# Head and tail of an attention layer: x loaded and summed first, and three products of the last but one group kept in PSUM

## The chip, the cores and the metric

The kernel runs on one core of a Trainium2 chip. The metric is device time in microseconds (us) of one execution. A core has a matrix engine (TensorE, PE in the profile, with PEld for its weight loads), a vector engine (VectorE, DVE), a scalar engine (ScalarE, ACT), GpSimd (POOL) and SyncE (SP). Each takes its own instructions in order; SP, ACT and POOL also issue DMAs. Matrix products are written to PSUM, a small memory of eight banks; everything else lies in SBUF.

## The reference

Input x is 8 x 256 x 512 in fp32. All that matters of the computation:

```python
xn = layernorm(x)                                   # over the last axis, eps 1e-5
q, k, v = xn @ wq.T, xn @ wk.T, xn @ wv.T           # 32 heads, 8 key/value heads of 128
q, k = rotary(q), rotary(k)
scores = q @ k.T / sqrt(128) * key_scale + causal   # 256 x 256 for each head
s = softmax(scores) @ v @ wo.T
logits = xn @ router_w.T                            # 4 experts, the best 2 of them kept
delta = sum_e gate_e * ((xn @ A_e.T) @ B_e.T) * 4   # rank 16
out = x + s * silu(delta)
```

## The kernel before

**Tiling.** Batches are taken two at a time: `tb` runs over 4 pairs (512 rows of x, four tiles of 128 rows), `g` over 8 groups of four heads, `b` over the two batches of a pair. Every large product (query, key, value, output projection) is done by a scheme of seven products in place of eight for a 2 x 2 block matrix (Strassen's, in Winograd's form). Its operands are blocks A11, A12, A21, A22 and sums of blocks S1 to S4 (S3 is written over A21), on both sides. One such set of weights is called a quad; 12 quads for each `tb` give queries, keys and values. Products of a quad are p1, p2, p6, p5, p7, p4, p3, each of four `nc.tensor.matmul` of 128 x 128 by 128 x 256, which are eight instructions in the profile.

**Head.** `norm(0)` (lines 318 to 478) loads four tiles of x through SP, takes mean and variance on VectorE (`statistics`, `variance`), the root on ScalarE (`root`), the reciprocal (`invert`) and the normalised tile (`normalise`) on VectorE, in two slices of two tiles. TensorE turns them (`turn`, one job for both tiles of a batch and one half of the columns; tile `xp`), ScalarE copies them out of PSUM (`read`; XB), and VectorE makes the four sums of x that the scheme needs (`add_up`; XT). `turn` serves the first pair only; later pairs are turned by VectorE and DMAs. Before it, TensorE multiplies the identity by itself (`warm`, line 1380). Weights of the first two quads come through SP (`blocks_of`, lines 482 to 545), those of all later ones through POOL; sums of weight blocks (`sum_up`, w<-w,w in the profile) are made on VectorE in the first pair and stored to DRAM by POOL (`keep_sum`, sums<-w) for the other three pairs. The router's products (`route`, four pieces, tile `lm`) and its weights (`ra`) belong to the head too. Weight tiles live in a ring of 9 (`w`) and 8 (`wo`), whose places are taken in a fixed turn.

**Middle.** For each group and batch: scores on TensorE (`sc`), softmax on VectorE and ScalarE, the probabilities turned by VectorE and two rounds of DMAs through DRAM (`there`, then `pT`), probabilities times values (`av`), and the output projection (`out_project`, line 930, `po`). The output projection has seven products for each group, and each product k has its own accumulator `acc[tb, k]` in SBUF, to which VectorE adds the product of each group (`add_up`, line 973; acc<-acc,po). Products take one of four PSUM banks tagged `mm`.

**Tail.** For the last pair's last group, `last_products` (line 1008) first adds accumulators into each other (`put`, seven sums in one chain), makes one of the four quarters of the output ready (`prepare(4, 1, 0)`: times gate, plus x), then runs the last seven products in PSUM banks `oa`, `oe`, `od` and two for halves of the seventh; ScalarE copies `oa` aside three times (p1, u2, u3), VectorE adds `oe` or `od` to these (`bank_and`), and `result` makes each quarter (plus accumulator, times gate, plus x: three operations), which SP stores.

**What sets the order.** All work is entered in a plan as jobs with an engine, an estimated duration, predecessors (`after`), rooms that they open and close (buffers of a tag, `Room` and `Hold`) and sometimes a job that they should be near to. The order of TensorE's jobs is laid out by hand (`lay`, lines 1362 and 1399 to 1446), which gives each a due time; due times of the other jobs are worked back from it (`Plan.run`, line 199), a job with `near` also taking that job's time as a limit. The plan then plays time forward with the estimated durations: whenever an engine is free, the ready job with the earliest due time, whose rooms have space, is emitted (jobs due more than 30 us after the earliest TensorE job not yet started are held back). A ready job with a late due time runs if nothing else is ready. The order found so is the program order of each engine on the chip; the waits there are real ones.

Nearly every instruction is recorded under line 118 (the helper that emits in program order), so tiles are named by their tensors in the profile.

## Time and profile before

| | us |
|---|---|
| runs of the kernel before | 1341.76, 1347.17, 1347.25 (median 1347.17) |
| the profiled execution | 1345.25 |
| its span, first to last instruction | 1343.5 |
| TensorE busy in the span | 1325.6 |
| VectorE busy in the span | 1102.8 |
| waits of TensorE for turned probabilities (`av` for `pT`) | 8.2, in 7 waits |
| start of the first product that needs a sum of x (`pdk<-XT,w`) | 15.94 |
| end of the last matmul | 1337.3 |
| end of VectorE's last operation | 1340.1 |

The profile is one execution. A line of the timeline gives start, time of the whole run of instructions, engine, operation, written and read tensors, and in brackets the engine's idle time just before it with what ended it. PE times are modelled at their ends: products that follow each other without a gap start 1.73 us apart, while a row of eight instructions shows 1.89 to 1.99.

### The profile page before, as it was taken

How to read it: one execution, taken by the hardware profiler on the slowest of the kernel's cores; microseconds unless marked ns; L12 is line 12 of the kernel's file. 1: busy time of each engine (PE TensorE's matmuls, PEld its weight loads, DVE VectorE, ACT ScalarE, POOL GpSimd, SP SyncE). 2: the span in 40 equal slices, each digit the busy share in tenths (PEclk: the TensorE clock that was granted, in tenths of full speed). 3: DMA queues.
4: the chain of work that ended last, by engine and by line, in shares of the span. 5: the costliest groups of instructions: out<-in, count | busy, mean ns of one | idle time of the engine just before them, and what ended most of it. 6: DMA issues, size and time to landing. Idle time of an engine off the chain costs nothing.

```text
span 1343.5 us, 19943 instructions
## 1 busy us (share of the span) xinstructions
PE 1325.6 (99%) x6488; PEld 1167.2 (87%) x6488; DVE 1102.8 (82%) x2835; ACT 611.2 (45%) x1576; POOL 314.3 (23%) x579
## 2 busy tenths in 40 slices
PE   9999999999999999999999999999999999999998
PEld 8888888888889888888888988888888898888886
DVE  6899989997978769788697875969868787686997
ACT  3474454543534435354353453535444454534531
POOL 2332232222222122221222212222122222222010
PEclk9999999999999999999999999999999999999999
DMA  6588677596766766768666676576876676666484
GB/s 212 165 264 253 203 217 226 197 261 205 244 178 199 223 202 185 232 210 221 205 223 202 214 208 216 175 236 210 227 221 191 220 219 205 191 189 199 137 282 135
DMA packets 134182, 282.10 MB, mean 210 GB/s; under 512 B 40832, under 2 KB 80896, under 8 KB 134080
## 3 DMA queue, kind: packets, MB, share of 16 engines
q0 software_dynamic: 45760, 149.98, 36.3%
q1 hardware_dynamic: 88096, 130.19, 31.7%
q8 instruction: 52, 0.85, 0.3%
q10 hardware_dynamic: 224, 0.66, 0.2%
q14 instruction: 50, 0.41, 0.1%
HBM read 197.94 MB, written 82.84 MB: 209 GB/s over the span
## 4 chain that ended last, share of the span: by engine, by line
PE 80%; DVE 10%; DMA 6%; SPq 2%; issue 1%; ACT 1%; DVEq 0%; ACTq 0%
PE po L118 21%; PE paq L118 15%; PE av L118 10%; PE sc L118 8%; PE pdq L118 7%; DMA pT<-there 5%; PE peq L118 4%; PE pak L118 4%; PE pav L118 4%; PE pdk L118 2%; SPq L118 2%; PE pdv L118 2%; DVE blocks L118 2%; DVE qTq L118 1%; DVE p L118 1%; DVE acc L118 1%
## 5 line engine op out<-in xcount | busy, mean ns | idle before, releaser
L118 ACT ACTIVATE p<-z,least 128x256 f32<-128x256 f32 (+7 forms) x512 | 207.6, 406 | 199.0 <-DVE least L118 130.3
L118 PE MATMUL po<-wo,a 128*128 128x256 f32 x992 | 233.0, 379 | 0.0
L118 PEld LDWEIGHTS po<-wo,a 128*128 128x128 f32 x992 | 186.7, 190 | 22.9
L118 PE MATMUL av<-pT,v 128*128 128x256 f32 x768 | 185.5, 380 | 8.2 <-DMA pT<-there 8.2
L118 PE MATMUL paq<-XT,w 128*128 128x256 f32 x768 | 182.0, 380 | 0.0
L118 DVE CUSTOM_DVE_ANT_0 z<-sc,tab 128x256 f32<-128x256 f32 (+7 forms) x512 | 134.1, 300 | 57.1 <-PE sc L118 54.1
L118 PE MATMUL po<-wo,s 128*128 128x256 f32 x744 | 177.6, 382 | 0.2 <-PE av L118 0.2
L118 PEld LDWEIGHTS av<-pT,v 128*128 128x128 f32 x768 | 145.0, 190 | 30.1 <-DMA pT<-there 6.1
L118 PEld LDWEIGHTS sc<-kk,qTq 128*128 128x128 f32 x1024 | 159.2, 191 | 12.6 <-DVE p L118 0.8
L118 PE MATMUL sc<-kk,qTq 128*128 128x256 f32 (+7 forms) x1024 | 168.0, 302 | 0.1
L118 PEld LDWEIGHTS paq<-XT,w 128*128 128x128 f32 x768 | 144.9, 190 | 19.5 <-ACT u2q L118 0.8
L118 POOL DMA_DIRECT2D w<-sums x144 | 79.2, 550 | 348.0 <-PE paq L118 143.9
L118 PEld LDWEIGHTS po<-wo,s 128*128 128x128 f32 x744 | 139.4, 190 | 23.4 <-issue 5.5
L118 ACT COPY a<-av 128x512 f32<-128x512 f32 x128 | 74.1, 580 | 180.8 <-PE av L118 180.6
L118 DVE TENSOR_TENSOR acc<-acc,po 128x512 f32<-128x512 f32 x189 | 127.7, 676 | 33.8 <-PE po L118 32.4
L118 ACT COPY swq<-cq 64x1024 f32<-64x1024 f32 x128 | 133.7, 1044 | 14.8 <-DVE cq L118 10.7
L118 POOL DMA_DIRECT2D w<-in_wquad_dram x148 | 80.9, 548 | 244.4 <-PE paq L118 84.6
L118 DVE STREAM_TRANSPOSE blocks<-p 128x1024 f32<-128x1024 f32 (+1 forms) x128 | 123.7, 968 | 0.4 <-DMA there<-blocks 0.2
L118 DVE TENSOR_SCALAR p<-p,total 128x256 f32<-128x256 f32 (+7 forms) x512 | 117.2, 294 | 2.3
L118 DVE TENSOR_TENSOR qTq<-cq,tab 128x1024 f32<-128x1024 f32 x64 | 77.9, 1218 | 26.2 <-ACT cq L118 26.0
L118 ACT ACTIVATION_READ_ACCUMULATOR p<-z,least 128x1 f32 x512 | 95.8, 187 | 0.0
L118 POOL DMA_DIRECT2D wo<-in_woquad_dram x104 | 56.9, 548 | 132.5 <-PE po L118 122.3
(137 smaller groups left out, 1853.3 us busy)
## 6 DMA issues: line engine op xcount, KB each, us to landing
there<-blocks SPq DMA_DIRECT2D x256, 192.0 KB, 3.8
pT<-there SPq DMA_DIRECT2D x64, 768.0 KB, 6.1
w<-in_wquad_dram POOLq DMA_DIRECT2D x148, 256.0 KB, 4.7
w<-sums POOLq DMA_DIRECT2D x144, 256.0 KB, 4.1
wo<-in_woquad_dram POOLq DMA_DIRECT2D x104, 256.0 KB, 5.0
wo<-osums POOLq DMA_DIRECT2D x96, 256.0 KB, 4.7
sums<-w POOLq DMA_DIRECT2D x48, 256.0 KB, 4.4
osums<-wo POOLq DMA_DIRECT2D x32, 256.0 KB, 4.7
```

What stands on the lines that cost most here:

```text
L118: ins = what(*args, **kwargs)
```

## The change

In the head:

- x tiles 2 and 3 are issued on SP after the first weight block (A11) instead of after the second.
- `variance` and `invert` are folded into `statistics` and `normalise`: the same instructions, in other jobs. Statistics and normalising jobs of one slice are put in a chain.
- The transposes of batch 0 are split by tile: those of tile 0, for both halves, may start when tile 0 is normalised. Estimated durations of these jobs are lower.
- The first sum of x waits for two of the four copies instead of all.
- Weight sums of the first quad are tied (`near`) to its product p3 instead of p1; in the other quads of the first pair to p1, as before.
- The four pieces of batch 0's transposes are laid ahead of the first product.

In the tail:

- Products 1, 2 and 5 of the last pair's last but one group (`fuse`) are not added to their accumulators. They stay in their PSUM banks, which become `oa`, `oe` and `od` of `last_products`, and the last group's products are accumulated on them.
- The order of that group's products becomes 1, 2, 6, 7, 5, 3, 4, and that of the last group 1, 5, 6, 2, 7, first half of 3, 4, second half of 3.
- The sums of accumulators are no longer one chain. All four quarters are prepared (times gate, plus x) ahead; `result` then multiplies the bank's value by the gate and adds the prepared accumulator.

The core of the diff:

```diff
-        def statistics(t):
+        def statistics(t, ts):
...
+            if t == ts.stop - 1:
+                nc.vector.tensor_scalar_add(box["r"][:, ts], box["mv"][:, ts, 1], EPS)
...
-        def normalise(t):
+        def normalise(t, ts):
+            if t == ts.start:
+                nc.vector.reciprocal(box["r"][:, ts], box["r"][:, ts])
...
             sts = [
-                add("dve", 0.9, lambda t=t: statistics(t), after=[loads[t]] + xn[-1:])
+                add("dve", 0.87, lambda t=t, ts=ts: statistics(t, ts),
+                    after=[loads[t]] + sts[-1:] + (xn[-1:] if t > 1 else []))
...
+            before, h = [], ph[2 * b + half]
+            if b == 0:
+
+                for f in range(2) if half == 0 else ():
+                    pieces.append(
+                        add("pe", 0.27, lambda f=f: turn(0, f, (0,)), after=[xn[0], identity],
+                            opens=[ph[f]], closes=mh[:1])
+                    )
+                before = [pieces[half]]
+            ts = (1,) if before else (0, 1)
...
-        t1 = add("dve", 0.61, lambda: add_up(0), after=reads)
-        t2 = add("dve", 0.61, lambda: add_up(1), after=[t1])
+        t1 = add("dve", 0.61, lambda: add_up(0), after=reads[0:3:2])
+        t2 = add("dve", 0.61, lambda: add_up(1), after=[t1] + reads)
...
-            if lead and k == 1:
+            if lead and k == 0:
                 plan.then(issue[0], first[2])
                 issue = first[3:]
...
-        if not tb:
-            for i in Features.sums:
-                sums_of["w", which, i].near = (p1, 0.0)
...
+        if not tb:
+
+            of = p1 if len(weights) > 1 else p3
+            for i in Features.sums:
+                sums_of["w", which, i].near = (of, 0.0)
...
+        fuse = (tb, g) == (NTB - 1, KV - 2)
...
+            if fuse and k in (1, 2, 5):
+
+                fused[k] = box, h, p
+                pieces[k] = p
+                return
...
-        return [pieces[k] for k in (1, 2, 6, 5, 7, 4, 3)]
+        return [pieces[k] for k in ((1, 2, 6, 7, 5, 3, 4) if fuse else (1, 2, 6, 5, 7, 4, 3))]
...
-        prepare(4, 1, 0)
+        for k, b, f in ((2, 0, 0), (3, 0, 1), (5, 1, 1), (4, 1, 0)):
+            prepare(k, b, f)
...
-            r = dve(
-                lambda: nc.vector.tensor_add(s(), s(), box[what]), turn + [first, M[k]["done"]]
-            )
-            m = dve(lambda: gate(s(), s(), b, f), [r, loads["g", b]])
+            m = dve(lambda: gate(box[what], box[what], b, f), [first, loads["g", b]])
             return dve(
-                lambda: nc.vector.tensor_add(s(), s(), box["xf", b][:, :, bass.ts(f, 2 * P)]),
-                [m, loads["xf", b]],
-            )
...
+                lambda: nc.vector.tensor_add(M[k]["s"], M[k]["s"], box[what]), [m, M[k]["done"]]
+            )
...
-        oa, oe, od, o3, o4 = (hold("mm") for _ in range(5))
-        p1 = product("oa", A11, A11, True, [], [oa])
+        oa, oe, od = (fused[k][1] for k in (1, 2, 5))
+        for k, bank in ((1, "oa"), (2, "oe"), (5, "od")):
+            fused[bank] = fused[k]
+        o3, o4 = (hold("mm") for _ in range(2))
+        p1 = product("oa", A11, A11, False, [])
...
-        return [p1, p2, p6, p5, p7, half(0, o3, p7), p4, half(1, o4, p4)]
+        return [p1, p5, p6, p2, p7, half(0, o3, p7), p4, half(1, o4, p4)]
...
-    lay(tiles[:2] + lead[:1] + tiles[2:] + lead[1:7] + route + lead[7:14] + turn + lead[14:])
+    lay(tiles[:4] + lead[:1] + tiles[4:] + lead[1:7] + route + lead[7:14] + turn + lead[14:])
```

More of the change, by code (lines that the diff above doesn't have):

```diff
@@ L341, in statistics @@
             nc.vector.bn_aggr(out=box["mv"][:, t, :], in_=st)
-        def variance(ts):
-            nc.vector.tensor_scalar_add(box["r"][:, ts], box["mv"][:, ts, 1], EPS)
+            if t == ts.stop - 1:
+                nc.vector.tensor_scalar_add(box["r"][:, ts], box["mv"][:, ts, 1], EPS)
         def root(ts):
             nc.scalar.sqrt(box["r"][:, ts], box["r"][:, ts])
-        def invert(ts):
-            nc.vector.reciprocal(box["r"][:, ts], box["r"][:, ts])
-        def normalise(t):
+        def normalise(t, ts):
+            if t == ts.start:
+                nc.vector.reciprocal(box["r"][:, ts], box["r"][:, ts])
             xn = box[t] = two.tile([P, D], F32, tag="m", name=f"xn{tb}_{t}")
@@ L357, in normalise, with turn @@
             )
-        def turn(b, half):
-            pt = box["p", b, half] = ps_mm.tile([P, 2, S], F32, tag="mm", name=f"xp{b}_{half}")
-            for t in range(2):
+        def turn(b, half, ts):
+            if ts[0] == 0:
+                box["p", b, half] = ps_mm.tile([P, 2, S], F32, tag="mm", name=f"xp{b}_{half}")
+            for t in ts:
                 for c in range(2):
                     nc.tensor.transpose(
-                        pt[:, c, bass.ts(t, P)], box[2 * b + t][:, bass.ts(2 * half + c, P)], ident
+                        box["p", b, half][:, c, bass.ts(t, P)], box[2 * b + t][:, bass.ts(2 * half + c, P)], ident
                     )
@@ L427, in norm @@
             begun.extend(issues)
-        xn = []
+        xn, sts = [], []
         for ts in [slice(0, NT)] if tb else [slice(0, 2), slice(2, NT)]:
@@ L432, in norm @@
             sts = [
-                add("dve", 0.9, lambda t=t: statistics(t), after=[loads[t]] + xn[-1:])
+                add("dve", 0.87, lambda t=t, ts=ts: statistics(t, ts),
+                    after=[loads[t]] + sts[-1:] + (xn[-1:] if t > 1 else []))
                 for t in tiles
             ]
-            v = add("dve", 0.1, lambda ts=ts: variance(ts), after=sts)
-            r = add("act", 2.8 if tb else 0.2, lambda ts=ts: root(ts), after=[v])
-            inv = add("dve", 0.1, lambda ts=ts: invert(ts), after=[r])
+            r = add("act", 2.8 if tb else 0.2, lambda ts=ts: root(ts), after=sts)
             for t in tiles:
                 xn.append(
-                    add("dve", 0.45, lambda t=t: normalise(t), after=[inv], opens=[mh[t]],
-                        closes=[xh[t // 2]])
+                    add("dve", 0.45, lambda t=t, ts=ts: normalise(t, ts), after=[r] + xn[-1:],
+                        opens=[mh[t]], closes=[xh[t // 2]])
                 )
@@ L456, in norm @@
         for b, half in [] if tb else ((0, 0), (0, 1), (1, 0), (1, 1)):
+            before, h = [], ph[2 * b + half]
[7 more added lines that the diff above has]
+            ts = (1,) if before else (0, 1)
             tp = add(
-                "pe", 0.9, lambda b=b, h=half: turn(b, h), after=xn[2 * b : 2 * b + 2] + [identity],
-                opens=[ph[2 * b + half]], closes=mh[2 * b : 2 * b + 2],
+                "pe", 0.27 * len(ts), lambda b=b, h=half, ts=ts: turn(b, h, ts),
+                after=xn[2 * b : 2 * b + 2] + [identity] + before,
+                opens=[] if before else [h], closes=mh[2 * b + ts[0] : 2 * b + 2],
             )
@@ L462, in norm @@
                 add("act", 0.5, lambda b=b, h=half: read(b, h), after=[tp] + reads[:1],
-                    opens=[] if reads else [x_hold[tb]], closes=[ph[2 * b + half]], near=(tp, 0.5))
+                    opens=[] if reads else [x_hold[tb]], closes=[h], near=(tp, 0.5))
             )
             pieces.append(tp)
-        t1 = add("dve", 0.61, lambda: add_up(0), after=reads)
-        t2 = add("dve", 0.61, lambda: add_up(1), after=[t1])
+        t1 = add("dve", 0.61, lambda: add_up(0), after=reads[0:3:2])
+        t2 = add("dve", 0.61, lambda: add_up(1), after=[t1] + reads)
         t3 = add("dve", 0.61, lambda: add_up(2), after=reads)
@@ L764, in values_of @@
         return pieces
-    free_p = [None]
+    fused = {}
     def softmax(tb, g, b):
@@ L1013, in last_products, with put @@
         dve = lambda what, after, **kw: add("dve", 0.61, what, after=after, **kw)
-        turn = []
-        def put(to, a, b):
-            turn[:] = [
-                dve(lambda: nc.vector.tensor_add(M[to]["s"], M[a]["s"], M[b]["s"]),
-                    turn + [M[k]["done"] for k in (to, a, b)])
-            ]
-            M[to]["done"] = turn[0]
-        for to, a, b in ((2, 1, 2), (6, 1, 6), (7, 6, 7), (3, 3, 5), (3, 3, 6), (4, 7, 4), (5, 7, 5)):
-            put(to, a, b)
+        puts = []
+        def put(to, a, b, after=()):
+            M[to]["done"] = dve(
+                lambda: nc.vector.tensor_add(M[to]["s"], M[a]["s"], M[b]["s"]),
+                [M[k]["done"] for k in (to, a, b)] + list(after),
+            )
+            puts.append(M[to]["done"])
+        put(2, 1, 2)
+        put(3, 3, 5)
+        read5 = puts[-1:]
+        put(6, 1, 6)
+        put(3, 3, 6)
+        put(7, 6, 7)
+        put(5, 7, 5, read5)
+        put(4, 7, 4)
         box, loads = {}, {}
@@ L1049, in prepare @@
             s = lambda: M[k]["s"]
-            m = dve(lambda: gate(s(), s(), b, f), [M[k]["done"], turn[0], loads["g", b]])
+            m = dve(lambda: gate(s(), s(), b, f), [M[k]["done"], loads["g", b]])
             M[k]["done"] = dve(
@@ L1054, in prepare @@
             )
-        prepare(4, 1, 0)
+        for k, b, f in ((2, 0, 0), (3, 0, 1), (5, 1, 1), (4, 1, 0)):
+            prepare(k, b, f)
         banks = {}
         def product(bank, a, w, first, after, opens=(), ts=(0, 1)):
+            before = fused.get(bank)
+            along = before and bank not in banks
+            if along:
+                banks[bank] = None
+                after = after + [before[2]]
             def work():
-                if first:
+                if along:
+                    banks[bank] = before[0]["ps"]
+                elif first:
                     banks[bank] = ps_mm.tile([P, 2, 2 * P], F32, tag="mm", name=f"{bank}{n}")
@@ L1097, in result @@
         def result(k, b, f, what, first):
-            s = lambda: M[k]["s"]
-            r = dve(
-                lambda: nc.vector.tensor_add(s(), s(), box[what]), turn + [first, M[k]["done"]]
-            )
-            m = dve(lambda: gate(s(), s(), b, f), [r, loads["g", b]])
-            return dve(
-                lambda: nc.vector.tensor_add(s(), s(), box["xf", b][:, :, bass.ts(f, 2 * P)]),
-                [m, loads["xf", b]],
-            )
-        oa, oe, od, o3, o4 = (hold("mm") for _ in range(5))
-        p1 = product("oa", A11, A11, True, [], [oa])
+            m = dve(lambda: gate(box[what], box[what], b, f), [first, loads["g", b]])
+            return dve(
+                lambda: nc.vector.tensor_add(M[k]["s"], M[k]["s"], box[what]), [m, M[k]["done"]]
+            )
+        oa, oe, od = (fused[k][1] for k in (1, 2, 5))
[3 more added lines that the diff above has]
+        p1 = product("oa", A11, A11, False, [])
         c1 = aside("p1", p1)
-        p2 = product("oe", A12, A21, True, [], [oe])
+        p6 = product("oa", S2, S2, False, [c1])
+        c6 = aside("u2", p6)
+        p2 = product("oe", A12, A21, False, [p6])
         e = bank_and("p1", "oe", [p2, c1], [oe])
         store(lambda: M[2]["s"], 0, 0, p2, [result(2, 0, 0, "p1", e)])
-        p6 = product("oa", S2, S2, False, [c1])
-        c6 = aside("u2", p6)
-        p5 = product("od", S1, S1, True, [], [od])
+        p5 = product("od", S1, S1, False, [])
         d = bank_and("u2", "od", [p5, c6], [od])
@@ L1125, in last_products @@
         m = dve(
-            lambda: gate(M[7]["s"], banks["oa"], 1, 0), [p4, M[7]["done"], turn[0], loads["g", 1]],
+            lambda: gate(M[7]["s"], banks["oa"], 1, 0), [p4, M[7]["done"], loads["g", 1]] + puts,
             closes=[oa],
@@ L1136, in half @@
                 lambda: gate(M[6]["s"][:, t, :], banks[bank][:, t, :], 0, 1, t),
-                [p, M[6]["done"], turn[0], loads["g", 0]], closes=[h],
+                [p, M[6]["done"], loads["g", 0]] + puts, closes=[h],
             )
```

## The prediction

> **What bounds the kernel now.** I read the page first (busy times, chain), then who waited for whom on TensorE, then the timeline of the first 20 us and of the last 45 us.

> The page's busy times and the chain that ended last, by engine:

> ```profile
> PE 1325.6 (99%) x6488; PEld 1167.2 (87%) x6488; DVE 1102.8 (82%) x2835; ACT 611.2 (45%) x1576; POOL 314.3 (23%) x579
> ...
> PE 80%; DVE 10%; DMA 6%; SPq 2%; issue 1%; ACT 1%; DVEq 0%; ACTq 0%
> ```

> TensorE is busy for 1325.6 of 1343.5 us, so at most 17.9 us can be had without taking matmuls away, and the change takes none away. Where these 17.9 us lie, the list of TensorE's waits says (us in total, times, longest):

> ```profile
> PE av L118 <- DMA pT<-there: 8.2, 7, 1.8
> PE warm L118 <- POOL ident masks.py:199: 1.4, 1, 1.4
> PE pdk L118 <- DVE XT L118: 1.0, 1, 1.0
> PE xp L118 <- DVE xn L118: 0.6, 2, 0.5
> PE pak L118 <- ACT XB L118: 0.2, 1, 0.2
> ```

> 8.2 us are waits for turned probabilities in the middle; the last three lines, 1.9 us, are the head; the rest is the tail, 1337.3 (last matmul) to 1343.5. The head, in the timeline:

> ```profile
> 6.90 1.09 PE L118 MATMUL xp<-ident,xn 128*128 128x128 f32 x8 [0.46 <-DVE xn L118]
> 7.59 1.07 ACT L118 COPY XB<-xp 128x512 f32<-128x512 f32 x2 [1.99 <-PE xp L118]
> 8.23 1.99 PE L118 MATMUL pak<-XB,w 128*128 128x256 f32 x8 [0.24 <-ACT XB L118]
> 8.61 0.69 DVE L118 BATCH_NORM_STATS2 st<-x 128x6 f32<-128x512 f32 x1 [1.76 <-DMA x<-in_x_dram]
> 11.98 2.61 DVE L118 TENSOR_TENSOR w<-w,w 128x512 f32<-128x512 f32 x4
> 15.11 1.28 DVE L118 TENSOR_TENSOR XT<-XB 128x512 f32<-128x512 f32 x2
> 15.94 1.96 PE L118 MATMUL pdk<-XT,w 128*128 128x256 f32 x8 [0.99 <-DVE XT L118]
> ```

> VectorE waits 1.76 us for the third x tile, then does four weight sums (2.61 us) before the first sum of x (XT) at 15.11, and TensorE waits for that. The tail:

> ```profile
> 1317.41 0.69 DVE L118 TENSOR_TENSOR acc<-acc,po 128x512 f32<-128x512 f32 x1 [3.42 <-PE po L118]
> 1319.14 0.69 DVE L118 TENSOR_TENSOR acc<-acc,po 128x512 f32<-128x512 f32 x1 [1.04 <-PE po L118]
> ...
> 1336.29 1.03 PE L118 MATMUL o<-wo,s 128*128 128x256 f32 x4
> ...
> 1339.10 1.01 DVE L118 TENSOR_TENSOR acc<-acc,acc 128x512 f32<-128x512 f32 x2
> ```

> VectorE idles 3.42 + 1.04 + 0.31 + 1.04 = 5.8 us between 1314 and 1322.6, then runs without a gap over 0.4 us to 1340.1, 2.8 us after the last matmul. After the last half product only two operations of 0.42 us and a 0.2 us hop are unavoidable (0.95 us: 1338.2), so 1.9 us of the tail are VectorE's backlog.

> **The head, step by step** (p1, p2, ... are the seven products of the first quad, 1.73 us apart in the trace).
> *Transposes by tile.* The same 16 transposes (0.137 us each). Those of x tile 0 need its normalised tile, done at 6.38, and the warming matmuls end at 6.44; four transposes run 6.44 to 7.0, beside the normalising of tile 1 (done 6.84). For the first copy two more remain, 7.0 to 7.25, plus the 0.14 us seen between transposes and copy: 7.4 for 7.59. So p1 starts at 8.03, p2 at 9.76, and TensorE is free at 11.5: 0.2 us earlier.
> *Loads.* On SP the order becomes x0, x1, A11, x2, x3, A12, ra, A21, A22 (ra is ready while A21 still waits one hop for A12). Landings before, issue plus time to landing: A11 6.7, A12 7.95, x2 8.6, x3 9.25, A21 10.0, ra 10.3, A22 10.9. I give x2 the place of A12, 7.95 (at best 7.3, one spacing of 0.65 behind A11), x3 8.6, A12 9.25. The chain from first statistics to the last normalised tile took 8.61 to 12.06 = 3.45, so that tile is done at 11.43, in time for TensorE at 11.5. A12 is wanted at 9.76: 0.5 us of cover. A21 is late by ra's 0.35, hidden, as the first weight sum needs A22 too. Epsilon and reciprocal move inside other jobs, same instructions: nothing.
> *Sums of x first.* The due times no longer pull the weight sums forward, so by the planner's rules VectorE does S1, the first output sum (needs p2), S2 and the first x sum in this order. x sum 0 needs only two of the four copies: transposes 11.5, copy 12.2 to 12.8. With 0.61 us a sum from 11.45: S1 12.05, output sum 12.65, S2 13.25, x sum 13.87, p5 at 14.0 instead of 15.94. But before, two router pieces (16 matmuls in 1.90) ran ahead of p5 and now one does; the other, 0.9, follows later, in a wait that the trace shows filled anyway. Gain 1.94 - 0.9 = 1.0; with x2 at 7.3 it is 1.3. I take 1.1.
> *What is moved behind.* S3 and S4 come up to 1.8 us later (three x sums ahead); on POOL the four stores of sums follow them and nobody waits for these. SP's next two weight loads wait for ring slots that S3 and S4 free (SP waited 5.1 us for VectorE there); their sums ran at 19.86 and are used by the product at 29.98, and VectorE is busy 7.4 of 10.5 us from 16 to 26.5: hidden. If the two table loads (0.96 us of ACT's queue, 10.55 to 11.51) fall between the copies of x, copy 3 is up to 0.5 late; it feeds x sum 1, which has all of p5 (1.73) as cover.
> Bounds of the head: 0, if A12 lands as late as A22 did, 10.9, 1.1 after it is wanted; 1.9, if every wait of TensorE's head goes.

> **The tail, step by step.** Count VectorE's operations from the first product of group (3,6) on. Before: 7 adds of its products, 7 sums of accumulators, 4 sums of the last group's activations, 2 for one prepared result, 3 bank sums, 9 for three results: 32, and six for the last two results. After: 4 adds (products 1, 2, 5 stay in PSUM), 7, 4, 8 for four prepared results, 3, and 6: 32 again, and the same six. So nothing is saved; operations move. Two of product 1's and 2's adds leave the busy stretch before 1313, and "prepare result 2" (2) fills the idle one.
> TensorE after 1312.8, no wait assumed: av (2.6), products 7, 5, 3 to 1320.5, p1 to 1322.2, av to 1324.8, product 4 to 1326.5, p5, p6, p2, p7, half, p4, half to 1337.2, where it ended before.
> VectorE: product 3's add at 1320.7, then three accumulator sums and two prepared results, 8 x 0.605 to 1325.6; four activation sums, product 4's add, its accumulator sum and prepared result, 8 x 0.605 from 1325.86 to 1330.7; bank sum and result 3, 2, 5, nine x 0.605 to 1336.2; then four halves at 0.335 and two whole at 0.605 to 1338.8, for 1340.1. Gain 1.3. The last store behind it (3.4 us to the end) is the same.
> *The added wait.* Three of the four "mm" banks are held from product 5 on. Product 4 must wait for product 3's add: 0.2 from matmul to add, 0.69 the add, 0.1 back, 0.97 in all. Its cover is p1 (needs a bank that is held already, an activation copied at 1315 and a weight issued at 1305.07) and the av behind it, whose pT was issued at 1315.41 and took 5.7: there at 1321.1. Were neither ready, products 3 and 4 would both wait: 1.9 us, TensorE ends at 1339.2, VectorE 0.95 later, at 1340.1 as before: gain 0. Upper bound 1.9, the whole backlog.
> [...] No row here shows a wait for a bank, and four pieces of other work stand ready, so I go by the rows.

> **The sum.** 1.1 + 1.3 = 2.4. The profiled execution took 1345.25 (span 1343.5 and 1.75 around it): 1342.85. The timed runs are 1341.76, 1347.17 and 1347.25, their median 1.9 above the profiled one; from the middle of the four, 1346.2, the forecast is 1343.8.

> **Rivals.**
> *The middle is put in another order, for the worse (other side).* The planner lays all engines' orders out once, and the head shifts its start. The middle holds seven waits for pT, 8.2/7 = 1.17 us each, at 60 to 120, 240 to 400, 600 to 700, 900 to 1000 us, where VectorE is 93% busy at first (222.6 of 240 from 60 to 300). For it: a later probability sum is late there at once. Against it: from the second quad on no cost or due time changes but a common shift. Each more costs 1.17; from the third more (3.5 over 2.4) the kernel is slower: four give 1346.2 - 2.4 + 4.7 = 1348.5. Over 0.5% takes eight.
> *The middle for the better.* Four fewer: 1346.2 - 2.4 - 4.7 = 1339.1.
> *A gain is eaten.* A12 late, or the bank waits showing: 1346.2 - 1.1 or - 1.3, about 1345; both eaten, 1346.2: the change then does nothing.

> **How the numbers follow.** Forecast 0.5; one or both gains eaten 0.2; middle worse 0.18; middle better 0.12. 0.5% of 1347.17 is 6.7 us, about what a measurement here can tell from none, as the three runs already lie 5.5 apart: the bounds are 1340.4 and 1353.9. Faster: middle better, 0.12, and 0.08 from low runs of the forecast: 0.2. Slower: half of "worse" at the most, 0.1. Same 0.7. Range: both upper bounds (3.8) and four waits fewer, 1346.2 - 3.8 - 4.7 = 1337.7; no gain and four more, 1350.9.

> **What would show it.** Head: third x tile's statistics at 7.3 to 8.0; first XT sum before S3 and S4, near 13.3; pdk near 14.0 after one router piece. Tail: no add for products 1, 2, 5; no idle of TensorE for a bank after 1315; VectorE's last operation within 1.8 us of the last matmul. Wrong if pek waits for A12, if TensorE shows gaps of 1 us before products 3 or 4, or if the pT waits leave 8.2 by more than 3 us.

## The result, and the profile after

The changed kernel is slower. Its median is 1347.06 us against 1343.94 us for the kernel before in the same session; the ratio is 1.0024, with a 95% interval from 1.0014 to 1.0034. The forecast was 2.4 us faster; the measurement is some 3.1 us slower, inside the given range and on the other side of no change. In absolute time the forecast started too high: its base was 1346.2, from the four runs there were, and 20 runs of before have their median at 1343.94.

The profiled execution took 1350.06 us, its span is 1348.3 us, against 1345.25 and 1343.5 before. Each profile is one execution, and the time differs from execution to execution (the 20 runs of after lie between 1342.97 and 1352.23 us): the profiled one of after is 3.0 us above its median, the one of before 1.3. So the profiles show where time goes, and the timed runs how much. The page's busy times and the chain that ended last, after:

```profile
PE 1327.3 (98%) x6488; PEld 1167.4 (87%) x6488; DVE 1103.1 (82%) x2835; ACT 612.1 (45%) x1576; POOL 315.1 (23%) x579
...
PE 76%; DVE 11%; DMA 8%; SPq 2%; ACT 1%; issue 1%; DVEq 0%; ACTq 0%
```

Read the first line against the span. TensorE's matmuls, the same 6488, take 1327.3 us instead of 1325.6: 1.7 us more. Its idle time is 1348.3 - 1327.3 = 21.0 us instead of 17.9: 3.1 us more. Together these are the 4.8 us between the two spans. The chain has less TensorE in it and more DMA (8% for 6%), so the idle time hangs on transfers. TensorE's list of waits says which (us in total, times, longest):

```profile
PE av L118 <- DMA pT<-there: 11.2, 8, 2.7
PE xp L118 <- DVE xn L118: 0.9, 1, 0.9
PE pak L118 <- ACT XB L118: 0.5, 1, 0.5
PE pdk L118 <- DVE XT L118: 0.3, 1, 0.3
```

The head's wait for the sums of x (`pdk` for XT) went from 1.0 to 0.3 us, as the edit meant. The waits for turned probabilities, pT, went from 8.2 to 11.2 us: almost all of the added idle time.

**The head did what was forecast.** Its timeline, after:

```profile
7.31 0.69 DVE L118 BATCH_NORM_STATS2 st<-x 128x6 f32<-128x512 f32 x1 [0.37 <-DMA x<-in_x_dram]
13.15 1.28 DVE L118 TENSOR_TENSOR XT<-XB 128x512 f32<-128x512 f32 x2
13.89 1.99 PE L118 MATMUL pdk<-XT,w 128*128 128x256 f32 x8 [0.34 <-DVE XT L118]
20.94 0.69 DVE L118 TENSOR_TENSOR ck<-pdk,u3k 128x512 f32<-128x512 f32 x1 [4.09 <-ACT u3k L118]
25.36 1.94 PE L118 MATMUL paq<-XB,w 128*128 128x256 f32 x8
```

The third x tile's statistics start at 7.31 (8.61 before), the first XT sum at 13.15 (15.11), `pdk` at 13.89 (15.94). All four router pieces are done in both kernels when q's first product `paq` starts, at 25.36 against 26.53: 1.17 us gained, and the first scores start 1.14 us earlier (46.8 for 48.0; here and below the second matmul of a unit's scores is taken). The fourth line is what I had not counted: VectorE now idles 4.09 us at 17 to 21 us and does work later that it did there, above all the second quad's weight sums (19.86 to 23.0 before, 25.35 to 29.6 after). From there the written-out order of every engine differs. Job for job, leaving out the first normalisation, 56 of TensorE's jobs, over 200 of VectorE's and 48 of POOL's stand in another place with the head's edits; with the tail's edits alone it is about ten, under 40 and none.

**The lead is gone at 78 us.** The first, second and fourth lines here are stores and loads on POOL, `there` and `pT` the two DMAs on SP that turn the probabilities, `av` their use; timeline of after:

```profile
58.37 1.15 POOL L118 DMA_DIRECT2D sums<-w  x2
59.52 1.64 POOL L118 DMA_DIRECT2D w<-in_wquad_dram  x3
61.05 3.55 SPq L118 DMA_DIRECT2D there<-blocks  x4
62.76 1.61 POOL L118 DMA_DIRECT2D osums<-wo  x3 [0.32 <-issue]
72.89 0.34 SPq L118 DMA_DIRECT2D pT<-there  x1
78.51 1.78 PE L118 MATMUL av<-pT,v 128*128 128x256 f32 x5 [2.71 <-DMA pT<-there]
```

The same transfers in the timeline of before:

```profile
67.64 3.09 SPq L118 DMA_DIRECT2D there<-blocks  x4
74.14 0.34 SPq L118 DMA_DIRECT2D pT<-there  x1
82.72 1.46 PE L118 MATMUL av<-pT,v 128*128 128x256 f32 x6
```

Before, the gather (`pT`) goes out 3.4 us after the last block store was issued (70.73 to 74.14) and its use comes 8.6 us later, without a wait. After, the stores go out 6.6 us earlier, into a pile of transfers of 256 KB each, and the gather goes out 8.3 us after the last of them (64.60 to 72.89). The planner allows 3.4 us for this step (its lag) in either case, and put the use ahead of the next unit's scores (a unit is one group of heads of one batch, written (tb, g, b)), where before had it behind the first of them: TensorE stands for 2.71 us. The stretches of the two kernels between 60 and 70 us, and the one behind the wait (us, busy time of each engine with its instructions, granted clock, DMA share, GB/s), after and then before:

```profile
60.00:70.00 10.00, 10.00 (x53) 9.04 (x52) 8.38 (x27) 5.74 (x15) 3.86 (x8) 1.00 0.98 320
76.10:79.50 3.40, 0.99 (x4) 0.91 (x5) 3.40 (x5) 0.33 (x1) 2.37 (x5) 0.97 0.87 306
79.50:82.90 3.40, 3.40 (x10) 2.66 (x10) 0.55 (x1) 0.59 (x1) 0.00 (x0) 0.53 0.85 240
```

```profile
60.00:70.00 10.00, 10.00 (x52) 8.19 (x52) 8.04 (x32) 6.08 (x16) 0.00 (x0) 1.00 0.35 119
```

The DMA engines are 98% busy instead of 35%. And behind the wait, from 79.5 to 82.9, TensorE is granted about half its clock (0.53): ten matmuls, where before has 19 in the same stretch. That is the 1.7 us of added busy time. A second wait, 2.43 us at 112, follows; before waits 1.53 us there. By 130 us the lead of 1.14 is a lag of 4.7 us; later waits, which before has at 290 to 390 us (1.33, 0.90, 1.83) and after nearly not (0.67), give most of it back: behind 390 us after is 1.1 us late. Up to the last unit's scores it falls to 4.1 us late again, partly by longer waits at 974 us (1.63 for 0.81) and 1176 us (0.57 for none).

**The tail** keeps TensorE's forecast order to the job, and no product waits for a bank: behind 1300 us TensorE's list of waits has 1.6 us for pT and 0.2 us of `po` for `av`, and nothing else. But the last gather does not come in time; after:

```profile
1304.84 0.71 SPq L118 DMA_DIRECT2D xf<-in_x_dram  x1
1305.60 0.86 SPq L118 DMA_DIRECT2D g<-gates  x1
1306.57 0.38 SPq L118 DMA_DIRECT2D xf<-in_x_dram  x1
1307.61 0.33 SPq L118 DMA_DIRECT2D pT<-there  x1
1318.24 2.83 PE L118 MATMUL av<-pT,v 128*128 128x256 f32 x12 [1.61 <-DMA pT<-there]
1341.77 1.03 PE L118 MATMUL o<-wo,s 128*128 128x256 f32 x4
1343.93 1.02 DVE L118 TENSOR_TENSOR acc<-acc,acc 128x512 f32<-128x512 f32 x2
```

VectorE ends 2.15 us behind TensorE (2.8 before), so its backlog shrank, though not to the 1.8 at most that was forecast. But three loads of 512 KB now stand on SP just ahead of the gather, which takes 10.5 us to land (7.4 before), and TensorE waits 1.61 us for it (0.28 before). The same gather and its use, before:

```profile
1305.33 0.33 SPq L118 DMA_DIRECT2D pT<-there  x1
1312.82 2.83 PE L118 MATMUL av<-pT,v 128*128 128x256 f32 x12 [0.28 <-DMA pT<-there]
```

From the last unit's first scores to the end of the span it is 51.6 us (50.9 before): the tail's gain is more than eaten.

### The profile page after: what moved, and what is told of

It reads as the page before. It is cut to its first block, busy times and chain, and to the rows that moved or that the text cites. A ratio compares the mean times of both kernels' runs of the same rounds, so it can differ in the third digit from the quotient of the medians.

```text
span 1348.3 us, 19942 instructions
## 1 busy us (share of the span) xinstructions
PE 1327.3 (98%) x6488; PEld 1167.4 (87%) x6488; DVE 1103.1 (82%) x2835; ACT 612.1 (45%) x1576; POOL 315.1 (23%) x579
## 4 chain that ended last, share of the span: by engine, by line
PE 76%; DVE 11%; DMA 8%; SPq 2%; ACT 1%; issue 1%; DVEq 0%; ACTq 0%
PE po L118 21%; PE paq L118 14%; PE av L118 10%; PE sc L118 7%; PE pdq L118 7%; DMA pT<-there 5%; PE pak L118 4%; PE pav L118 4%; PE peq L118 3%; DMA there<-blocks 2%; PE pdk L118 2%; DVE blocks L118 2%; SPq L118 2%; DVE p L118 2%; PE pdv L118 2%; DVE acc L118 1%
## 5 line engine op out<-in xcount | busy, mean ns | idle before, releaser
L118 ACT ACTIVATE p<-z,least 128x256 f32<-128x256 f32 (+7 forms) x512 | 208.4, 409 | 191.8 <-DVE least L118 129.6
L118 PE MATMUL po<-wo,a 128*128 128x256 f32 x1024 | 240.7, 379 | 0.0
L118 PEld LDWEIGHTS po<-wo,a 128*128 128x128 f32 x1024 | 192.5, 190 | 23.8 <-ACT u L118 0.2
L118 PE MATMUL av<-pT,v 128*128 128x256 f32 x768 | 187.0, 383 | 11.2 <-DMA pT<-there 11.2
L118 PE MATMUL paq<-XT,w 128*128 128x256 f32 x768 | 181.9, 380 | 0.2 <-ACT u3q L118 0.2
L118 PE MATMUL po<-wo,s 128*128 128x256 f32 x760 | 181.2, 382 | 0.6 <-DVE s L118 0.4
L118 DVE CUSTOM_DVE_ANT_0 z<-sc,tab 128x256 f32<-128x256 f32 (+7 forms) x512 | 134.3, 301 | 57.4 <-PE sc L118 54.5
L118 PEld LDWEIGHTS av<-pT,v 128*128 128x128 f32 x768 | 146.0, 191 | 34.2 <-DMA pT<-there 8.2
L118 PEld LDWEIGHTS sc<-kk,qTq 128*128 128x128 f32 x1024 | 159.6, 191 | 11.5
L118 PE MATMUL sc<-kk,qTq 128*128 128x256 f32 (+7 forms) x1024 | 167.6, 302 | 0.0
L118 PEld LDWEIGHTS po<-wo,s 128*128 128x128 f32 x760 | 142.2, 190 | 24.8 <-issue 5.3
L118 POOL DMA_DIRECT2D w<-sums x144 | 79.2, 550 | 361.3 <-PE paq L118 147.0
L118 PEld LDWEIGHTS paq<-XT,w 128*128 128x128 f32 x768 | 145.0, 190 | 20.0 <-ACT p L118 0.8
L118 DVE TENSOR_TENSOR acc<-acc,po 128x512 f32<-128x512 f32 x186 | 126.1, 678 | 36.7 <-PE po L118 35.3
L118 ACT COPY a<-av 128x512 f32<-128x512 f32 x128 | 74.3, 582 | 180.0 <-PE av L118 179.8
L118 ACT COPY swq<-cq 64x1024 f32<-64x1024 f32 x128 | 134.0, 1047 | 15.1 <-DVE cq L118 10.9
L118 POOL DMA_DIRECT2D w<-in_wquad_dram x148 | 81.2, 550 | 236.6 <-PE paq L118 85.5
L118 DVE STREAM_TRANSPOSE blocks<-p 128x1024 f32<-128x1024 f32 (+1 forms) x128 | 124.1, 971 | 0.2
L118 DVE TENSOR_SCALAR p<-p,total 128x256 f32<-128x256 f32 (+7 forms) x512 | 117.6, 296 | 2.3
L118 DVE TENSOR_TENSOR qTq<-cq,tab 128x1024 f32<-128x1024 f32 x64 | 78.1, 1220 | 27.8 <-ACT cq L118 27.8
L118 ACT ACTIVATION_READ_ACCUMULATOR p<-z,least 128x1 f32 x512 | 97.0, 189 | 0.0
L118 POOL DMA_DIRECT2D wo<-in_woquad_dram x104 | 57.0, 549 | 146.1 <-PE po L118 136.2
```

The lines of the kernel that those rows point to most:

```text
L118: ins = what(*args, **kwargs)
```

## The experiments

The first theory: the head's edits cost the time, by the order that the planner lays out behind them, and the tail's edits are worth about 1 us if the loads at the end do not stand before the gather. The rivals: the tail loses the time, or one part of the head does (x ahead of the second weight block, or transposes and sums).

**The head's edits alone, the tail's edits alone, and the tail's with the loads brought forward.** The first two take the respective half of the change; the third adds a due time to the end's loads of gates and x:

```diff
-            loads[what, b] = add("sp", 0.3, work, after=after, opens=[hold(tag)], lag=9.0)
+            loads[what, b] = add(
+                "sp", 0.3, work, after=after, opens=[hold(tag)], near=(fused[1][2], -14), lag=9.0
+            )
```

> Only the head's edits; the tail is that of the kernel before. Theory A (the head's edits shift the written-out order of the first groups; the new order sends a burst of transfers into the turning of the first probabilities, TensorE waits some 2.7 us at about 78 us and the granted clock halves for 3.4 us behind it): the first scores 1.1 us earlier than before, first scores of the sixth unit 4 to 5 us later, in all 2 to 4 us slower than before. Theory B (the head brings its 1.1 us, the loss comes from the tail: PSUM banks, loads): 1 us faster.

> Only the tail's edits; the head is that of the kernel before. Theory A: no wait of the middle changes; the tail gains 0.6 us in VectorE's backlog and loses 1.3 us to a longer wait for the turned probabilities of the last group, whose gather now stands on SP behind three loads of 512 KB: 0.5 to 1 us slower than before, near the bound of what can be told. Theory B: 3 to 4 us slower.

> The tail's edits, with the four loads of gates and x given a due time 14 us ahead of the first kept product, so that none stands on SP between the last group's first spread and its gather. If the loads are what delays that gather: its landing comes back to about 7.4 us after the issue (10.5 in the changed kernel), TensorE's last wait for it to 0.3 us (1.6), and the kernel is 0.5 to 1.3 us faster than before, 1.3 faster than the tail alone. If not: as the tail alone.

Measured: head alone 1.0017 [1.0003, 1.0031], slower; tail alone 0.9992 [0.9977, 1.0007], no difference; tail with early loads 0.9988 [0.9974, 1.0002]. So most of the loss sits in the head's edits. Theory A had the tail alone 0.5 to 1 us slower than before, with 1.3 us more of wait for the last gather; it did not come out so, and that wait is 0.89 us in its profile. In the head's profile the waits for pT are 0.90 us at 77 and 2.62 at 109, then half clock from 109.4 to 112.9, and the lead of 0.93 at the first scores is a lag of 3.4 in the last unit. In the third kernel's timeline the last two gathers on SP have no load ahead of them,

```profile
1302.83 0.34 SPq L118 DMA_DIRECT2D pT<-there  x1
1307.18 2.43 SPq L118 DMA_DIRECT2D there<-blocks  x4
1313.86 0.34 SPq L118 DMA_DIRECT2D pT<-there  x1
```

no wait for pT is left behind 1300 us, and from the last unit's first scores to the end it is 49.8 us: 1.1 less than before, for 1.3 forecast. That is read from the traces; the interval still touches no change.

**One part of the head each, and later use of pT.** The first kernel below takes only the loads of x ahead of the second weight block and the sums of x ahead of the weight sums; the second only the transposes by tile, with epsilon and reciprocal inside the neighbouring jobs; the third is the whole head, but the planner is told that unit (0,0,0)'s blocks take longer to land; the fourth is the first with the tail and its early loads.

```diff
-        out_ = add("sp", 2.4, spread, after=[t1], closes=[bh], near=(sc, 5.0), lag=3.4)
+        out_ = add("sp", 2.4, spread, after=[t1], closes=[bh], near=(sc, 5.0),
+                   lag=9.4 if (tb, g) == (0, 0) else 3.4)
```

> Of the head's edits only three: x tiles 2 and 3 ahead of the second weight block, the weight sums due by p3, the first sum of x behind two copies; transposes, their jobs and their estimated durations as before. The written-out order of TensorE then differs from before in 12 places, all among its first 60 jobs, and POOL's order is unchanged. Theory A (the head's gain is real and the loss is the order of the first groups): first scores some 1 us earlier, and this lead is still there in the seventh unit; 1 us faster than before (ratio 0.999). Rival (any earlier start of the sums of x brings the pile of transfers at 60 to 70 us, whatever the order): 2 to 3 us slower, as the whole head.

> Of the head's edits only the others: transposes by tile, jobs folded and chained, lower estimated durations; loads and weight sums as before. TensorE's order differs from before in 19 places, POOL's in 19. Theory A: the first scores at most 0.5 us earlier, the order of the first groups close to that before: within 0.1% of before. Rival (the lower estimated durations alone are what turns the plan over): 2 to 3 us slower.

> The whole changed head, and the plan is told that the first group's probabilities take 6 us longer through DRAM (the trace of the changed kernel had 8.75 us where the plan has 3.4), so that it lays other products ahead of the first av products. The transfers themselves stay in the same pile. Theory A, with the wait itself as the cost: TensorE's 2.7 us wait near 78 us shrinks under 1 us; 1.5 to 3 us faster than the changed head alone, so within 1 us of before. Rival (the pile of transfers costs through something else than that wait): as the changed head alone, 1.0017.

> The three edits of the head that leave the first groups' order almost alone, the whole tail, and the tail's loads due 14 us earlier. Theory A: both gains add, 1 us of the head and 1.1 to 1.5 of the tail: 2 to 2.5 us faster than before (ratio 0.998), 5 faster than the changed kernel. Rival (gains of the head and the tail are lost in the middle whatever the order): no faster than before.

Measured, in that order: 1.0010 [0.9996, 1.0023], 1.0012 [0.9998, 1.0025], 1.0012 [0.9997, 1.0027], 0.9991 [0.9980, 1.0001]. None can be told from no change, so the times do not say which part of the head does it, and the later use of pT shows no gain over the whole head (1.0017). The fourth kernel, for 2 to 2.5 us expected, came out some 1.2 us below before. The traces say more. With x first alone the wait before `pdk` stays, 1.31 us, and the first scores come only 0.2 us earlier (1 expected); with the transposes alone they come 1.4 us earlier (at most 0.5 expected). Each reaches the middle with another order and loses the lead at another place: both wait at 641 us (2.70 and 2.44 us) and are granted half clock right behind it. The fourth kernel waits 2.45 us for pT at 393 us, with half clock behind it, and 2.11 at 974. With the later use of pT the waits for it at 78 and 112 us are gone; other pieces wait there, 0.7 us (a product, at 78) and 1.3 us (`po` for sums, at 107), and its list of waits begins

```profile
PE av L118 <- DMA pT<-there: 2.8, 3, 1.9
```

and that execution's span is 1340.1 us. So moving one use of pT in the plan takes away the waits at the place where after lost its lead. It does not show a gain in time: the twelve runs lie between 1340.94 and 1350.90 us with a median of 1346.27, and the profiled one, 1341.89, is among the fastest.

**The whole change with both repairs, the pile taken away, and a wait by itself.** The second kernel ties the first output group's weight sums, and so their four stores on POOL, to the gather of unit (0,0,0) (`gathers[tb, g, b] = in_` in `softmax`); the third is the kernel before with one unit's block stores issued four times.

```diff
-                after=[there[a], there[b]] + form.before(i, there) + (loaded["xn"] if first else []),
+                after=[there[a], there[b]] + form.before(i, there) + (loaded["xn"] if first else [])
+                + ([gathers[0, 0, 0]] if room == "wo" and key == 0 else []),
...
-            for h in range(G):
+            for h in list(range(G)) * (4 if (tb, g, b) == (0, 6, 0) else 1):
```

> The whole change, with the plan's lag for unit (0,0,0)'s turned blocks raised from 3.4 to 9.4 and the loads of gates and x for the end brought forward. Theory (what was lost is one misplaced use of pT at 78 us, its follower at 112, and the loads in front of the last gather): no wait over 1.5 us at 78 and 112 us, first scores 1.2 us earlier than before, no wait for pT behind 1300 us, 49.8 us from the last unit's first scores to the end; 2 to 3 us faster than before, about 1341. Rival (the other waits for pT, which recur in every kernel and change from run to run, decide): 1343 to 1345, no different from before.

> The whole change, but the first output group's four weight sums, and with them their four stores of 256 KB, come after the gather of unit (0,0,0); the lag stays at 3.4, the use of pT stays where the change put it. If the pile of stores beside the turned blocks makes pT late: blocks land within 4 to 6 us instead of 8.75 and the wait at 78 us falls from 2.71 to under 1. If the use is simply too early whatever lies beside it: the wait stays over 2.

> The kernel before, with the four stores of turned blocks of unit (0,6,0) issued four times over (the same bytes each time), so that its pT comes about 7 us later; nothing else is changed. It prices one wait of TensorE alone. pT was 3 to 4 us early, so a wait of 3 to 4 us is expected near 274 us. If a wait costs its own length: 3 to 4 us slower than before. If the clock drops behind it for one stretch of 3.41 us at half speed, as behind the waits of 2.7 us seen so far: 1.7 us more, 5 to 6 us slower. If later waits absorb it: under 2.

Measured: both repairs 0.9995 [0.9981, 1.0008]; no pile 1.0029 [1.0016, 1.0041]; the made wait 1.0082 [1.0068, 1.0096].

The two repairs bring the change from 1.0024 to 0.9995, back to the kernel before, and no further: the theory that they would leave it 2 to 3 us faster fell, and its rival's 1343 to 1345 held (1343.11). Each mark named ahead was met (0.68 us of wait at 78, 0.71 at 107, none for pT behind 1300 us, 49.8 us at the end); waits for pT at 307, 391 and 640 us are left, of 1.04, 2.11 and 1.39.

Without the four stores, the timeline and the waits of that kernel are

```profile
61.26 2.83 SPq L118 DMA_DIRECT2D there<-blocks  x4
69.69 0.34 SPq L118 DMA_DIRECT2D pT<-there  x1
75.85 2.75 PE L118 MATMUL av<-pT,v 128*128 128x256 f32 x12
```

```profile
PE av L118 <- DMA pT<-there: 8.9, 7, 3.5
```

The gather goes out 5.6 us after the last block store (8.3 with them), 3.2 us earlier on the clock, and the wait at 78 us is gone: the stores made pT late there. But the time is no better than the change's. TensorE now waits 3.53 us at 109 and is granted half clock behind it. A wait taken away at one place came back at the next.

The made wait was larger than meant, as the repeated stores waited for each other (SP stood 11.1 us for them): 15.2 us of issuing, a wait of 10.8 us that ends at 317.1 us, for 3 to 4 expected. In stretches of 3.4 us:

```profile
304.50:307.90 3.40, 1.81 (x9) 1.25 (x7) 0.00 (x0) 0.00 (x0) 0.00 (x0) 1.00 0.67 172
307.90:311.30 3.40, 0.00 (x0) 0.00 (x0) 0.98 (x1) 0.00 (x0) 0.00 (x0) 0.96 0.97 202
311.30:314.70 3.40, 0.00 (x0) 0.00 (x0) 3.22 (x14) 1.79 (x8) 0.00 (x0) 0.50 0.84 157
314.70:318.10 3.40, 0.99 (x2) 0.84 (x3) 3.16 (x6) 1.55 (x5) 0.00 (x0) 0.50 0.96 368
318.10:321.50 3.40, 3.40 (x10) 2.73 (x9) 3.40 (x6) 0.58 (x1) 0.54 (x1) 0.53 0.48 80
```

Against before, this kernel goes from 1.9 us ahead (scores at 301 us in before) to 10.1 behind (at 335): 12.0 us. The wait is 9.9 us longer than before's 0.9 at that place, and from 317.1 to 321.3 TensorE works 4.2 us at half clock, 2.1 us: 12.0. So this wait cost its length and half of the time that TensorE worked at half clock behind it. In the last unit it is still 9.5 us behind, so next to nothing is absorbed later; the timed ratio, 9.1 to 12.9 us, agrees.

**A longer lag for every gather.** The waits at 110, 290, 310, 391, 641 and 972 us recur in most of these kernels, before among them (the one at 110 is put down to ScalarE's `p` in some). The next theory: the planner's 7.0 us for a gather is too short for what lies beside it. (A longer lag there covers a late store as well, since the use waits for both steps: at 78 us in after it was the stores that were late, 8.3 us for 3.4, while the gather itself landed in 5.6.) Both kernels have the tail and its early loads; the second also has the head.

```diff
-        in_ = add("sp", 0.35, gather, after=[out_], opens=[th], lag=7.0)
+        in_ = add("sp", 0.35, gather, after=[out_], opens=[th], lag=10.0)
```

> The kernel before with the tail's edits, the end's loads of gates and x brought forward, and the plan's lag for the gather of turned blocks raised from 7.0 to 10.0 for all 64 units, so that each use of pT stands one to four pieces later. If the waits that recur at 110, 290, 310, 391, 641 and 972 us come from too short a lag: their sum falls from 8 us to under 3, no stretch of half clock, and with the tail's 1.1 the time is 5 to 8 us below before, 1337 to 1340. If the orders that follow bring new waits as the head's did: 1342 to 1345, and the list of waits shows them at other places.

> The whole change with the same lag of 10.0 for all gathers and the end's loads brought forward. If the lag cures what the head lost: the waits at 78 and 112 us are under 1 together, first scores are 1.1 us earlier, and it is 1 us faster than the run without the head's edits beside it, 1336 to 1339. If the head's own order loses time in another way: 1 to 3 us slower than that run.

Measured: 1340.19 us, 0.9968 [0.9959, 0.9978], without the head; 1340.18 us, 0.9967 [0.9955, 0.9979], with it. Both are faster than before. All waits for pT are gone; without the head the list of waits begins

```profile
PE pak L118 <- DMA XB<-turned: 3.1, 1, 3.1
PE po L118 <- DVE s L118: 1.6, 1, 1.6
```

One wait took their place: for the turned x of the second row block, at 295 us. The expected cure hit; the amount, 5 to 8 us, came short by this wait. The head brought nothing that this pair can show: its means differ by 0.2 us, and from the spread of its 10 and 6 runs that is good to about 1.3.

**The same lag for turned x.** Again without and with the head:

```diff
                     add("sp", 2.4, lambda b=b: gather(b), after=[out_] + reads[:1],
-                        opens=[] if b else [x_hold[tb]], lag=7.0)
+                        opens=[] if b else [x_hold[tb]], lag=11.0)
```

> As the kernel with the lag of 10.0 for all gathers (tail's edits, the end's loads early, no edit of the head), and the plan's lag for the gathers of turned x raised from 7.0 to 11.0. If the wait of 3.1 us at 295 us comes from too short a lag too: it is under 0.5, no stretch of half clock behind it, 2 to 4 us faster than 1340.2, so 1336 to 1338. If the later order only moves it: a wait of 2 to 3 us elsewhere before 340 us and 1339 to 1341.

> The same with the head's edits, so the whole change with both lags and the end's loads early. If the head's gain is real once what follows is covered: first scores 0.4 us earlier than in the run beside it and 0.4 to 1.1 us faster, 1335 to 1337. If the gain is lost in the order behind it: no faster than the run beside it, with a longer stall between the first scores and 130 us.

Measured: 1336.78 us (1336.08 to 1337.27), 0.9931 [0.9916, 0.9946], without the head; 1335.70 us (1335.45 to 1336.21), 0.9924 [0.9907, 0.9940], with it. This is the fastest kernel of the study; before's median in its session is 1346.52, so both kernels of this case are beaten. Its waits and its chain:

```profile
PE po L118 <- DVE s L118: 1.6, 1, 1.6
PE warm L118 <- POOL ident masks.py:199: 1.4, 1, 1.4
PE pak L118 <- ACT XB L118: 0.5, 1, 0.5
PE pdk L118 <- DVE XT L118: 0.3, 1, 0.3
PE paq L118 <- ACT u3q L118: 0.2, 1, 0.2
```

```profile
PE 98%; DVE 1%; ACT 0%; issue 0%; POOL 0%; DVEq 0%; POOLq 0%
```

TensorE waits for no transfer behind its start, the chain is TensorE for 98%, and the clock is never halved between the head and the last matmul. Two things follow. The head is worth 0.9 us (the means, 1336.69 and 1335.76, with an interval of about 0.6 either way from the spread of the five runs each) once what it moves is covered: near the 1.1 of the forecast. And the runs of one kernel lie within 1.2 and 0.8 us of each other, where the nine of before spread over 6.4 in the same session: the uncovered waits, it seems, were also what made the time vary. What is left is the last line of work of the tail: `po` waits 1.6 us for the last group's sums, and with it the end is as long as before's, some 50.9 us from the last unit's first scores. I did not try to mend it.

## Why the prediction was wrong

Step by step, by its own terms:

- *Head, 1.1.* Right in size and mechanism: 1.17 us at q's first product, the third tile's statistics at the early edge of the 7.3 to 8.0 given, XT and `pdk` within 0.2 us of the forecast, A12 in time. (For a third tile that early the prediction's own figure was 1.3.)
- *"What is moved behind ... hidden".* Half right. TensorE waits for none of the weight sums that moved (0.24 us at 35 us, for an activation). But what moved on POOL with them, stores and loads of 256 KB, met the block stores of the first unit. The step counted who waits for these transfers and not which transfers they lie beside.
- *"From the second quad on no cost or due time changes but a common shift."* This is the step that failed, and it carried the low chance, 0.18, of the rival that came true in kind. A common shift of due times is not a common shift of an order: free slots, idle engines and ready times change with the head, and the planner takes the next ready job. The place was the right one (VectorE full, first units), the price was wrong in two ways: the two waits were 2.7 and 2.4 us (none and 1.5 before), not 1.17 each, and the first brought 1.7 us of half clock with it. In number there was one wait for pT more, 8 for 7, not the three more from which the prediction had the kernel turn slower; their sum left 8.2 by 3.0 us, just on the prediction's own sign of being wrong. The premise is not quite true of the diff either: `statistics`, `variance` and `invert` have other estimates in the later pairs too. No run tells what that alone does.
- *Tail, 1.3.* Mechanism right: order to the job, no wait for a bank (going by the rows was right here), backlog down from 2.8 to 2.15, where 1.8 at the most was forecast. The size is 1.1 with the loads early. As changed it was lost to the last gather. The added wait that I looked for was the one for a bank; the one that came, of SP's loads ahead of SP's gather, follows from product 2's prepared result coming later, which gives its loads a later due time. I costed the moved operations of VectorE and not the due times of the DMAs that feed them.

What stays open: why precisely the planner lets the first output group's loads go in one piece of four at 47 us after the head's edits, where before had one and three, was not taken apart. Nor do the runs say how the part of the head with the transposes and the one with x share the loss; each alone is within the noise. And the longer lags were not run on the kernel before by itself, without the tail's edits.

## What to carry to other kernels

Where one planner lays out all queues, a saving at the start is a new order for all that follows; before costing it, look for the transfers whose allowed time is already too short (here waits for pT in 7 places before the change), since these decide what the new order costs. Mending them first, by two numbers in the plan, was worth some 7 to 8 us (0.9931 with them against 0.9988 without, both with the tail and its early loads and without the head); only then could the 1 us of the edit itself be measured. And of moved work, list the transfers that it issues and what lies beside them, not only who waits for them.

## What the hardware showed that I had not expected

```profile
290.20:293.60 3.40, 1.70 (x14) 1.56 (x12) 2.97 (x17) 2.94 (x12) 0.00 (x0) 1.00 1.02 223
293.60:297.00 3.40, 2.00 (x9) 1.82 (x10) 2.82 (x9) 0.94 (x6) 0.00 (x0) 1.00 1.00 233
297.00:300.40 3.40, 3.40 (x17) 2.99 (x16) 1.60 (x6) 1.63 (x2) 1.10 (x2) 1.00 0.94 183
```

With the head it is 3.0 us, most of it in one, and the next is at half clock:

```profile
292.90:296.30 3.40, 1.50 (x7) 1.32 (x8) 3.37 (x14) 1.35 (x8) 0.00 (x0) 0.96 1.02 233
296.30:299.70 3.40, 3.40 (x10) 2.75 (x9) 0.10 (x1) 1.63 (x2) 0.55 (x1) 0.53 0.91 172
```

Each such stretch costs 1.7 us on top of the wait, half of 3.41, where TensorE works through it, as in after, where TensorE is busy for 1.7 us more than in before.
